# Messages' products directly behind the distances, and the first batch's imaginary parts added by TensorE

## The chip, the cores and the metric

The kernel runs on one core of a Trainium2 chip. The metric is the device time of one execution in microseconds, the median of several. Names used below: TensorE (PE in the profile) multiplies matrices into PSUM, whose banks of 512 numbers per partition the kernel takes from a pool of eight; VectorE (DVE), ScalarE (ACT) and GpSimd (POOL) work on what lies in SBUF and PSUM (GpSimd on SBUF alone); SyncE's queue (SP) issues most of the loads. Each engine has its own list of instructions, which the program writes by hand in a fixed order, and works through it from the front.

## The reference

There are 64 graphs of 256 nodes with 256 features. Layer 0 has three branches per graph, a convolution along the nodes (17 taps), a message passing with weights from distances, and a GRU that joins them; layer 1 is a graph convolution. Cut to what matters here:

```python
# layer 0
h = relu(bn(conv1d(x, conv1_w)))                  # 1 tap
h = bn(conv1d(h, conv2_w, pad=8))                 # 17 taps
x_conv = relu(h + x)
s    = x @ w_se.T + b_se                          # 3 numbers per node
dist = |s_n|^2 + |s_m|^2 - 2 s_n . s_m
A    = exp(-dist) * adj
msg  = relu(x @ w_msg.T + b_msg)
x_nmp = A @ msg
gi = concat(x_conv, x_nmp) @ w_ih.T + b_ih ;  gh = x @ w_hh.T + b_hh
r, z = sigmoid(gi_r + gh_r), sigmoid(gi_z + gh_z)
n = tanh(gi_n + r * gh_n)
x = layernorm(x + (1 - z) * n + z * x)
# layer 1
h = layer_norm(x) * gamma + beta
conv = (adj @ h) @ W_rel + b_rel + h @ W_root
x = layernorm(x + x + relu(conv))
```

## The kernel before

The 17-tap convolution is done for a batch of 8 graphs at a time by a polynomial transform: the nodes are cut into pieces, VectorE splits them into 15 complex "leaves" and two real ones (additions and multiply-adds, `split` and `merge`), TensorE multiplies each complex leaf with three filters, and VectorE puts the results together again. Of the three products of a leaf, k1 is the one of the sum of both parts; the real part is k1 minus the third product and the imaginary part is k1 plus the second. Two leaves share a bank per kind:

```python
    psum = ctx.enter_context(tc.tile_pool(name="psum", bufs=8, space=bass.MemoryType.PSUM))
    def bank(name):
        return psum.tile([P, 512], F32, tag="ps", name=name)

    def product(ps, slot, w, m):
        for c in range(C):                         # C = 2
            nc.tensor.matmul(ps, X[:, slot, c * P:(c + 1) * P], w(m, c), start=(c == 0), stop=(c == C - 1))   # L385

    def products(b, first, sums):
        p1, p2, p3 = bank("ps_k1"), bank("ps_k2"), bank("ps_k3")
        re, im, _ = LEAVES[first]
        for k in range(2):
            w = load_w(b, 3 * (first + k), 3)
            at = slice(k * D, (k + 1) * D)
            product(p1[:, at], sums + k, w, 0)
            product(p2[:, at], re + k, w, 1)
            product(p3[:, at], im + k, w, 2)
        def take():
            k1 = sl(sums, 2).rearrange("p s e -> p (s e)")
            nc.scalar.copy(k1, p1)                                                        # L400
            nc.vector.tensor_sub(sl(re, 2).rearrange("p s e -> p (s e)"), k1, p3)         # L401
            nc.vector.tensor_add(sl(im, 2).rearrange("p s e -> p (s e)"), k1, p2)         # L402
        return take
```

In the trace each float32 matmul is two instructions, so that `products` is 24 of them. `conv(b)` is a generator, which runs these pieces little by little: `take = products(...)`, some VectorE work, `take()`, and so on with the next pair of leaves. The first batch (b = 0) runs alone at the start, with the filters kept in SBUF; seven pairs and one odd group (`last_products`) are multiplied one after the other. It ends so:

```python
        if b == 0:
            def turned_x(q): ...         # 16 transposes of x into two banks (L541), left open for more
            yield None
            held = [turned_x(q) for q in range(3)]
        yield from butterflies([...])    # additions, L362
        for j in range(2): ...           # multiply-adds, L104
        ...
            for q in range(4):
                yield from second(q); yield from third(q); yield from third(q + 4)        # multiply-adds, L104
                pss = held.pop(0)
                ...                      # 16 transposes of the convolution's result onto x (L576)
                ...                      # relu by ScalarE (L581)
                if q == 1:
                    held.append(turned_x(3))
                yield None
```

The message part of a graph k, and the early calls for graphs 0 to 2:

```python
    def messages(k, idle=False):                   # idle: bias by TensorE, relu and copy by ScalarE
        ...
        for m in range(C):
            ps = bank("ps_msg")
            for c in range(C):
                nc.tensor.matmul(ps[:, :D + 4], XT[k][:, c, m * P:(m + 1) * P], wms[:, c, :], ...)   # L649
            if idle:
                ...
                continue
            nc.vector.tensor_add(twice[:, m, :, 0:3], ...)                 # L656, the 3 numbers s
            nc.vector.tensor_add(MSG[k][:, m, :], ps[:, :D], bms[:, :D])   # L658
        if not idle:
            nc.scalar.activation(MSG[k], MSG[k], AF.Relu)                  # L660
        ...                                        # five small GpSimd steps: -|s|^2 (L664 to L668)

    def factors(k): ...      # transposes of s (L675), two ScalarE copies
    def distances(k): ...    # two banks ps_dist, 2 products (L687), exponentials by ScalarE (L689)
    def mask(k): ...         # A = exp * adj by VectorE (L692)
    def passing(k): ...      # A @ msg (L699), copy by ScalarE

    while STAGE.get(0) != "inverse":               # the first batch's products
        if next(first) is None:
            count += 1
            if count == 3:   messages(0, True)
            elif count == 4: messages(1, True)
            elif count == 5: factors(0)
            elif count == 6: distances(0)
    messages(2, True)
    ...
    early = {2: lambda: factors(1), 3: lambda: mask(0), 4: lambda: passing(0)}
    for i, _ in enumerate(first):                  # the rest of the first batch
        if i in early:
            early[i]()
    distances(1)
    mask(1)
```

The main loop goes through the graphs of a batch, while `pump()` lets the next batch's convolution go on by its share. The end of an item (one graph k):

```python
            gates_n(k, 1)                  # bank ps_n, added by VectorE (L730)
            pump()
            project(k - 1)                 # two banks ps_out (L884), held until the aggregation
            distances(k + 2)
            step(up)                       # update: nn by VectorE twice, tanh by ScalarE
            pump()
            step(up)                       # update: w (from L839 on), statistics
            pump()
            messages(k + 3)
            step(up)                       # update: normalized h and x1
            pump()
            mask(k + 2)
            agg = aggregate(k - 1)         # L896 into the banks ps_out, added by VectorE (L898)
            step(agg)
            step(agg)
            pump()
```

Of the kernel before, what the change touches and what calls it, by code (L numbers as in the profile page):

```python
# [16 lines left out]
P = 128  # L17
# [59 lines left out]
def gnn_two_layers(  # L77
# [22 lines left out]
    def bank(name):  # L100
        return psum.tile([P, 512], F32, tag="ps", name=name)
# [278 lines left out]
        nc.sync.dma_start(out=t[:, :n], in_=w2m[first:first + n].rearrange("f c p o -> p f c o"))  # L380
        return lambda m, c: t[:, m, c, :]

    def product(ps, slot, w, m):
        for c in range(C):
            nc.tensor.matmul(ps, X[:, slot, c * P:(c + 1) * P], w(m, c), start=(c == 0), stop=(c == C - 1))  # L385

    def products(b, first, sums):

        p1, p2, p3 = bank("ps_k1"), bank("ps_k2"), bank("ps_k3")
        re, im, _ = LEAVES[first]  # L390
        for k in range(2):
# [8 lines that stand above are left out]
            nc.scalar.copy(k1, p1)  # L400
            nc.vector.tensor_sub(sl(re, 2).rearrange("p s e -> p (s e)"), k1, p3)  # L401
            nc.vector.tensor_add(sl(im, 2).rearrange("p s e -> p (s e)"), k1, p2)  # L402
        return take

    def last_products(b):
# [29 lines left out]
    def conv(b):  # L435
# [98 lines left out]
        if b == 0:  # L534

            def turned_x(q):
                xb = FIRST["xb"][q] if q < 3 else x_by_tiles(b, slice(q, M, 4))
                pss = [bank("ps_xc") for _ in range(C)]
                for o in range(C):
                    for j in range(4):  # L540
                        nc.tensor.matmul(pss[o][:, j * P:(j + 1) * P], xb[:, j, o * P:(o + 1) * P], ident,  # L541
                                         start=(j == 0), stop=False)
                return pss

            yield None
            held = [turned_x(q) for q in range(3)]
        yield from butterflies([(S2, U, U + 1, 1, True), (S2 + 1, U, U + 1, 1, False),
                                (U, S2, U + 2, 2, True), (U + 2, S2, U + 2, 2, False)])
        for j in range(2):
            stt(sl(S2 + j, 2, 2), sl(U + 4 + j, 2, 2), s4[j], sl(U + j, 2, 2))  # L550
            yield cost(2)
            stt(sl(S2 + 4 + j, 2, 2), sl(U + 4 + j, 2, 2), -s4[j], sl(U + j, 2, 2))
            yield cost(2)
# [14 lines left out]
        if b == 0:  # L568
            for q in range(4):
                yield from second(q)  # L570
                yield from third(q)
                yield from third(q + 4)
                pss = held.pop(0)
                for o in range(C):
                    for j in range(4):
                        nc.tensor.matmul(pss[o][:, j * P:(j + 1) * P], X[:, V + q + 4 * j, o * P:(o + 1) * P], ident,  # L576
                                         start=False, stop=(j == 3))
                for o in range(C):
                    pv = pss[o].rearrange("p (j g t) -> p j g t", j=4, g=BG)
                    for h in range(2):  # L580
                        nc.scalar.activation(xcs[h][:, o].rearrange("p g (t j) -> p j g t", j=M)[:, q::4],  # L581
                                             pv[:, :, 4 * h:4 * h + 4, :], AF.Relu)
                if q == 1:
                    held.append(turned_x(3))
                yield None
            return
        for j in range(4):
# [53 lines left out]
    def messages(k, idle=False):  # L641

        MSG[k] = ahead.tile([P, C, D], F32, tag="msg", name="msg", bufs=3)
        st = sts[k % len(sts)]
        twice = st.rearrange("p m (r e) -> p m r e", e=SR)
        for m in range(C):
            ps = bank("ps_msg")
            for c in range(C):
                nc.tensor.matmul(ps[:, :D + 4], XT[k][:, c, m * P:(m + 1) * P], wms[:, c, :],  # L649
                                 start=(c == 0), stop=(c == C - 1 and not idle))  # L650
            if idle:
                nc.tensor.matmul(ps[:, :D + 4], ones[0:1, :], bms[0:1, :], start=False, stop=True)
                nc.scalar.copy(twice[:, m, :, 0:3], ps[:, D:D + 3].unsqueeze(1).to_broadcast([P, 2, 3]))
                nc.scalar.activation(MSG[k][:, m, :], ps[:, :D], AF.Relu)
                continue
            nc.vector.tensor_add(twice[:, m, :, 0:3], ps[:, D:D + 3].unsqueeze(1).to_broadcast([P, 2, 3]),  # L656
                                 bms[:, D:D + 3].unsqueeze(1).to_broadcast([P, 2, 3]))
# [4 lines that stand above are left out]
        sq = ahead.tile([P, C, 3], F32, tag="sq", name="sq", bufs=2)  # L662
        ns = ahead.tile([P, C], F32, tag="ns", name="ns", bufs=3)
        nc.gpsimd.tensor_mul(sq, st[:, :, 0:3], st[:, :, 0:3])  # L664
        nc.gpsimd.tensor_add(ns, sq[:, :, 0], sq[:, :, 1])
        nc.gpsimd.tensor_add(ns, ns, sq[:, :, 2])
        nc.gpsimd.tensor_scalar(twice[:, :, :, 3], ns.unsqueeze(2).to_broadcast([P, C, 2]), -0.5, None, ALU.mult)
        nc.gpsimd.tensor_scalar(ns, ns, -1.0, None, ALU.mult)  # L668
        ST[k] = (st, ns)

    def factors(k):
        st, ns = ST[k]
# [35 lines left out]
    def gates_rz(k, n):  # L708
        if n == 0:
            RZ[k] = (work.tile([P, C, 2 * D], F32, tag="rz", name="rz", bufs=1),  # L710
                     work.tile([P, C, 2 * D], F32, tag="gn", name="gn", bufs=1))
        q, ins = inputs(k, n)
        prz = bank("ps_rz")
        for c in range(C):
            nc.tensor.matmul(prz, XT[k][:, c, q], whh[:, c, 0:2 * D], start=(c == 0), stop=False)  # L715
        for i, t in enumerate(ins):
            nc.tensor.matmul(prz, t, wih[:, i, 0:2 * D], start=False, stop=(i == 3))  # L717
        rz = RZ[k][0]

        nc.vector.tensor_add(rz[:, n, :], prz, brzn[:, :2 * D])  # L720
        nc.scalar.activation(rz[:, n, :], rz[:, n, :], AF.Tanh, scale=0.5)  # L721
# [379 lines left out]
    while STAGE.get(0) != "inverse":  # L1101
        if next(first) is None:
            count += 1
            if count == 3:
                messages(0, True)
            elif count == 4:
                messages(1, True)
            elif count == 5:
                factors(0)
            elif count == 6:  # L1110
                distances(0)
    messages(2, True)
    first_pool.close()

    work = ctx.enter_context(tc.tile_pool(name="work", bufs=2))
# [5 lines left out]
    nc.gpsimd.tensor_add(brzn[:, :2 * D], brzn[:, :2 * D], bhh)  # L1121
    load_x(0)

    early = {2: lambda: factors(1), 3: lambda: mask(0), 4: lambda: passing(0)}
    for i, _ in enumerate(first):
        if i in early:
            early[i]()
    distances(1)
    mask(1)

    POINTS = 10
# [3 lines left out]
    for b in range(NB):  # L1135
# [19 lines left out]
        for k in range(b * BG, min((b + 1) * BG, B - 1)):  # L1155
            load(k + 3)
            load_x(k + 1)
            up = update(k)
            agg = None
            gates_rz(k, 0)  # L1160
            pump()
            gates_n(k, 0)
            step(y_left)
            pump()
            if k > 0:
                transposes_h(k - 1)
            pump()
            gates_rz(k, 1)
            pump()
            if k + 1 < B:  # L1170
                passing(k + 1)
            pump()
            if k + 2 < B:
                factors(k + 2)
            gates_n(k, 1)
            pump()
            if k > 0:
                project(k - 1)
            if k + 2 < B:
                distances(k + 2)  # L1180
            step(up)
            pump()
            step(up)
            pump()
            if k + 3 < B:
                messages(k + 3)
            step(up)
            pump()
            if k + 2 < B:
                mask(k + 2)  # L1190
            if k > 0:
                agg = aggregate(k - 1)
# [3 lines that stand above are left out]
            y_left = agg  # L1196
# [7 lines left out]
    for k in range(first_k, B - 1):  # L1204
# [15 lines left out]
        project(k - 1)  # L1220
        if k + 2 < B:
            distances(k + 2)
        step(up)
        step(up)
        if k + 2 < B:
            block_sums(k + 1, 1)
        if k + 3 < B:
            messages(k + 3)
        step(up)
        if k + 2 < B:  # L1230
            mask(k + 2)
# [48 lines left out]
```

## Time and profile before

| | |
|---|---|
| median of 3 runs | 2248.66 us (2246.59 to 2248.96) |
| span of the profiled run | 2246.3 us |
| TensorE clock granted | 0.998 |
| mean DMA rate over the span | 101 GB/s |
| instructions | 24617 |

In the groups of instructions a line gives the source line, the engine, what is written from what, the shape, the number, the busy time and the mean of one. Those of the parts in question:

```profile
L649 PE MATMUL ps_msg<-wms,xT 128*128 128x260 f32 x512 | 131.4, 394 | 20.3 <-DVE XF L401 20.3
L699 PE MATMUL ps_nmp<-AT,msg 128*128 128x256 f32 x512 | 121.1, 379 | 0.0
L385 PE MATMUL ps_k<-w,XF 128*128 128x256 f32 x1316 | 294.2, 381 | 3.2 <-DMA w<-w2m 1.9
```

The last numbers are the time that the engine stood idle just before such instructions, and what ended it. A matmul's duration is that of one instruction through the pipe; in a stream the next one starts earlier than this one ends, so the time that TensorE needs is read from the starts. The chain of work that ended last runs for 84% of the span over TensorE and for 12% over VectorE.

### The profile page before, as it was taken

What the parts mean: (1) busy time and instruction counts of PE and PEld (TensorE: products, weight loads), DVE (VectorE), ACT (ScalarE), POOL (GpSimd) and SP (SyncE); (2) the same over time, 40 slices, a digit from 0 to 9 for tenths busy, and PEclk for the clock granted to TensorE, in tenths of its full rate; (3) what the DMA queues carried; (4) which work ended last, traced back from release to release, by engine and by line L of the source; (5) the groups of instructions that cost most, each with busy time, mean ns of one, the idle gap of its engine ahead of it and who ended that gap; (6) DMA issues with size and microseconds to landing.
All of it is one profiled execution on the core that took longest, in us unless ns stands there. A gap on an engine that the chain in (4) does not pass through costs nothing.

```text
span 2246.3 us, 24617 instructions
## 1 busy us (share of the span) xinstructions
PE 2202.2 (98%) x8400; PEld 1463.0 (65%) x8400; DVE 1721.5 (77%) x3329; ACT 769.2 (34%) x1587; POOL 511.7 (23%) x933
## 2 busy tenths in 40 slices
PE   8999999999999999999999999999999999999998
PEld 5775666656665666656666667666666667666664
DVE  6976889389882998749886598956989479896675
ACT  6423222532235322443224432244222432224333
POOL 0102212231221321223212321222212232222112
PEclk9999999999999999999999999999999999999999
DMA  5932433214423153232522244221432314421110
GB/s 149 316 111 69 141 103 98 96 46 140 136 76 103 38 164 108 78 106 80 164 64 84 92 132 131 70 97 64 142 111 83 103 54 141 131 81 38 43 33 19
DMA packets 212682, 226.69 MB, mean 101 GB/s; under 512 B 22103, under 2 KB 203854, under 8 KB 212558
## 3 DMA queue, kind: packets, MB, share of 16 engines
q1 hardware_dynamic: 190128, 191.27, 26.6%
q10 hardware_dynamic: 22430, 33.86, 4.3%
q8 instruction: 67, 1.10, 0.2%
q14 instruction: 57, 0.47, 0.1%
HBM read 179.22 MB, written 45.88 MB: 100 GB/s over the span
## 4 chain that ended last, share of the span: by engine, by line
PE 84%; DVE 12%; DMA 1%; issue 1%; POOL 1%; ACT 1%; SPq 0%; POOLq 0%; ACTq 0%; DVEq 0%
PE ps_rz L717 16%; PE ps_k L385 10%; PE ps_rz L715 8%; PE ps_n L729 8%; PE ps_out L884 7%; PE ps_c L468 5%; PE ps_nmp L699 5%; PE ps_msg L649 5%; PE ps_out L896 4%; PE ps_n L727 4%; DVE XF L104 4%; PE ps_w L230 2%; PE ps_dist L687 1%; DMA w<-w2m 1%; PE ps_hT L871 1%; DVE w L104 1%
## 5 line engine op out<-in xcount | busy, mean ns | idle before, releaser
L104 DVE SCALAR_TENSOR_TENSOR XF<-XF 128x512 f32<-128x512 f32 (+2 forms) x800 | 507.6, 665 | 7.4
L848 POOL TENSOR_SCALAR q<-mv 128x2 f32<-128x2 f32 x63 | 45.5, 723 | 1395.1 <-DVE mv L827 1395.1
L385 PE MATMUL ps_k<-w,XF 128*128 128x256 f32 x1316 | 294.2, 381 | 3.2 <-DMA w<-w2m 1.9
L385 PEld LDWEIGHTS ps_k<-w,XF 128*128 128x128 f32 x1316 | 247.9, 190 | 44.3 <-PE ps_n L729 6.2
L884 PE MATMUL ps_out<-wrr,hT 128*128 128x512 f32 x504 | 226.6, 592 | 0.0
L721 ACT ACTIVATE rz<-rz 128x512 f32<-128x512 f32 x114 | 71.9, 630 | 450.0 <-DVE rz L720 442.3
L730 DVE TENSOR_TENSOR gn<-ps_n,brzn 128x512 f32<-128x512 f32 x114 | 78.3, 687 | 181.3 <-PE ps_n L729 181.3
L715 PE MATMUL ps_rz<-whh,xT 128*128 128x512 f32 x456 | 214.5, 593 | 0.0
L717 PE MATMUL ps_rz<-wih,nmp 128*128 128x512 f32 x456 | 214.3, 592 | 0.0
L717 PE MATMUL ps_rz<-wih,xc 128*128 128x512 f32 x456 | 214.3, 592 | 0.0
L660 ACT ACTIVATE msg<-msg 128x512 f32<-128x512 f32 x61 | 38.4, 630 | 379.3 <-DVE msg L658 379.3
L720 DVE TENSOR_TENSOR rz<-ps_rz,brzn 128x512 f32<-128x512 f32 x114 | 77.6, 681 | 117.8 <-PE ps_rz L717 117.7
L717 PEld LDWEIGHTS ps_rz<-wih,xc 128*128 128x128 f32 x456 | 86.6, 190 | 109.1 <-issue 108.8
L717 PEld LDWEIGHTS ps_rz<-wih,nmp 128*128 128x128 f32 x456 | 86.6, 190 | 109.1 <-issue 109.1
L884 PEld LDWEIGHTS ps_out<-wrr,hT 128*128 128x128 f32 x504 | 95.3, 190 | 93.3 <-issue 81.3
L649 PE MATMUL ps_msg<-wms,xT 128*128 128x260 f32 x512 | 131.4, 394 | 20.3 <-DVE XF L401 20.3
L649 PEld LDWEIGHTS ps_msg<-wms,xT 128*128 128x128 f32 x512 | 92.6, 189 | 54.7 <-DVE XF L401 26.0
L362 DVE TENSOR_TENSOR XF<-XF 128x512 f32<-128x512 f32 (+3 forms) x128 | 126.2, 1010 | 1.7
L699 PE MATMUL ps_nmp<-AT,msg 128*128 128x256 f32 x512 | 121.1, 379 | 0.0
L715 PEld LDWEIGHTS ps_rz<-whh,xT 128*128 128x128 f32 x456 | 82.1, 190 | 57.7 <-issue 54.5
L896 PE MATMUL ps_out<-hr,adj 128*128 128x256 f32 x504 | 119.5, 380 | 0.0
L468 PE MATMUL ps_c<-xTc,w 128*128 128x512 f32 x256 | 116.7, 599 | 2.4 <-ACT xTc L458 2.3
(197 smaller groups left out, 3769.9 us busy)
## 6 DMA issues: line engine op xcount, KB each, us to landing
w<-w2m SPq DMA_DIRECT2D x105, 768.0 KB, 5.7
xn<-in_x_dram SPq DMA_DIRECT2D x32, 512.0 KB, 4.3
xt<-xTc ACTq DMA_DIRECT2D x32, 512.0 KB, 3.4
xT<-xt SPq DMA_DIRECT2D x64, 256.0 KB, 2.9
xb<-in_x_dram SPq DMA_DIRECT2D x32, 512.0 KB, 6.4
adj<-in_adjT_dram SPq DMA_DIRECT2D x64, 256.0 KB, 2.7
x<-in_x_dram SPq DMA_DIRECT2D x64, 256.0 KB, 3.0
out_dram<-y ACTq DMA_DIRECT2D x63, 256.0 KB, 2.2
```

Of the source, the lines that this page charges most:

```text
L104: nc.vector.scalar_tensor_tensor(o, in0, s, in1, op0=op0, op1=op1)
L362: (nc.vector.tensor_add if add else nc.vector.tensor_sub)(sl(o, n), sl(a, n), sl(b, n))
L385: nc.tensor.matmul(ps, X[:, slot, c * P:(c + 1) * P], w(m, c), start=(c == 0), stop=(c == C - 1))
L468: nc.tensor.matmul(pss[o], w1[:, c, o * P:(o + 1) * P], xTc[:, c, :], start=(c == 0), stop=(c == C - 1))
L649: nc.tensor.matmul(ps[:, :D + 4], XT[k][:, c, m * P:(m + 1) * P], wms[:, c, :], start=(c == 0), stop=(c == C - 1 and not idle))
L699: nc.tensor.matmul(ps[:, d * N:(d + 1) * N], MSG[k][:, m, d * P:(d + 1) * P], AT[k][:, m, :], start=(m == 0), stop=(m == C - 1))
L715: nc.tensor.matmul(prz, XT[k][:, c, q], whh[:, c, 0:2 * D], start=(c == 0), stop=False)
L717: nc.tensor.matmul(prz, t, wih[:, i, 0:2 * D], start=False, stop=(i == 3))
L727: nc.tensor.matmul(pn[:, D:], XT[k][:, c, q], whh[:, c, 2 * D:], start=(c == 0), stop=(c == C - 1))
L729: nc.tensor.matmul(pn[:, :D], t, wih[:, i, 2 * D:], start=(i == 0), stop=(i == 3))
L884: nc.tensor.matmul(ps, hT[:, c, n * P:(n + 1) * P], wrr[:, c, :], start=(c == 0), stop=(c == C - 1))
L896: nc.tensor.matmul(po, ADJ[k][:, m, n * P:(n + 1) * P], hr[:, m, :], start=False, stop=(m == C - 1), skip_group_check=True)
```

## The change

It has three parts. In the main loop, and in the last batch's loop, `messages` becomes a generator of two steps: the products come directly behind the distances, and the additions, the relu and the GpSimd steps come after the first pump, before the second step of the update. That is meant to take the products out of the place where they wait for a bank. In the first batch, the second product of a pair of leaves is accumulated onto k1 in its bank after k1 has been copied, so that the imaginary part is a copy by ScalarE in place of an addition by VectorE, and a pair takes two banks. And the early work of the first batch is put into another order, so that TensorE has something to do while VectorE finishes that batch. For graph 0 the GRU's products with the messages come before those with the convolution.

```diff
-    def product(ps, slot, w, m):
+    def product(ps, slot, w, m, first=True):
         for c in range(C):
-            nc.tensor.matmul(ps, X[...], w(m, c), start=(c == 0), stop=(c == C - 1))
+            nc.tensor.matmul(ps, X[...], w(m, c), start=first and c == 0, stop=(c == C - 1), skip_group_check=True)

     def products(b, first, sums):
+        if b == 0:
+            return products_added(first, sums)
...
+    def products_added(first, sums):
+        p1, p3 = bank("ps_k1"), bank("ps_k3")
+        re, im, _ = LEAVES[first]
+        w = [load_w(0, 3 * (first + k), 3) for k in range(2)]
+        at = [slice(k * D, (k + 1) * D) for k in range(2)]
+        k1 = sl(sums, 2).rearrange("p s e -> p (s e)")
+        for k in range(2):
+            product(p1[:, at[k]], sums + k, w[k], 0, k == 0)
+        nc.scalar.copy(k1, p1)
+        for k in range(2):
+            product(p3[:, at[k]], im + k, w[k], 2)
+        for k in range(2):
+            product(p1[:, at[k]], re + k, w[k], 1, False)
+        def take():
+            nc.scalar.copy(sl(im, 2).rearrange("p s e -> p (s e)"), p1)
+            nc.vector.tensor_sub(sl(re, 2).rearrange("p s e -> p (s e)"), k1, p3)
+        return take
...
-            held = [turned_x(q) for q in range(3)]
+            held = [turned_x(0)]
         yield from butterflies([...])
+        if b == 0:
+            FIRST["passing"]()                       # mask(0), passing(0)
+            held += [turned_x(q) for q in range(1, 3)]
...
                 if q == 1:
                     held.append(turned_x(3))
+                elif q == 2:
+                    FIRST["distances"]()             # distances(1)
...
     def messages(k, idle=False):
-        for m in range(C):
-            ps = bank("ps_msg")
+        pss = [bank("ps_msg") for _ in range(C)]
+        for m, ps in enumerate(pss):
             (products)
+        yield
+        for m, ps in enumerate(pss):
             (additions; behind them the relu and the GpSimd steps)
+        yield
...
-        for i, t in enumerate(ins):
-            nc.tensor.matmul(prz, t, wih[:, i, 0:2 * D], start=False, stop=(i == 3))
+        for j, i in enumerate((2, 3, 0, 1) if k == 0 else range(4)):
+            nc.tensor.matmul(prz, ins[i], wih[:, i, 0:2 * D], start=False, stop=(j == 3))
...
-            if count == 3:
-                messages(0, True)
-            elif count == 4:
-                messages(1, True)
+            if count == 4:
+                all_of(messages(0, True))
...
-    messages(2, True)
+    all_of(messages(1, True))
+    all_of(messages(2, True))
...
-    early = {2: lambda: factors(1), 3: lambda: mask(0), 4: lambda: passing(0)}
-    (the rest of the first batch with these calls in between; then distances(1))
+    factors(1)
+    (the rest of the first batch, with passing(0) and distances(1) inside it)
     mask(1)
...
             distances(k + 2)
+            msg = messages(k + 3) if k + 3 < B else None
+            step(msg)
             step(up)
             pump()
+            step(msg)
             step(up)
             pump()
-            if k + 3 < B:
-                messages(k + 3)
             step(up)
             pump()
```

The loop of the last batch is changed in the same way, without pumps.

## The prediction, made before the changed kernel was run

> **What bounds the kernel now.** I read the busy times first, then the waits of TensorE alone, then its timeline around each wait with VectorE's timeline for the same microseconds. TensorE bounds it:
>
> ```profile
> PE 2202.2 (98%) x8400; PEld 1463.0 (65%) x8400; DVE 1721.5 (77%) x3329; ACT 769.2 (34%) x1587; POOL 511.7 (23%) x933
> ...
> PE ps_msg L649 <- DVE XF L401: 20.3, 14, 1.6
> PE ps_xc L576 <- DVE XF L104: 3.4, 1, 3.4
> ```
>
> The change adds and removes no matmul, so it can win only time in which TensorE stands still, and the reader sees in lines 2 and 3 that little of that is there: 14 waits of the message products (the columns are total, number, longest) and one wait in the first batch. The first of the 14, and the second, which is shaped a little differently, in TensorE's timeline:
>
> ```profile
> 282.12 0.70 PE L687 MATMUL ps_dist<-lr 4*128 4x256 f32 x4
> 282.75 5.45 PE L385 MATMUL ps_k<-w,XF 128*128 128x256 f32 x24
> 288.03 1.04 PE L649 MATMUL ps_msg<-wms,xT 128*128 128x260 f32 x4
> 290.68 1.14 PE L649 MATMUL ps_msg<-wms,xT 128*128 128x260 f32 x4 [1.60 <-DVE XF L401]
> ...
> 325.14 0.70 PE L687 MATMUL ps_dist<-lr 4*128 4x256 f32 x4
> 325.77 5.45 PE L385 MATMUL ps_k<-w,XF 128*128 128x256 f32 x24
> 331.05 1.04 PE L649 MATMUL ps_msg<-wms,xT 128*128 128x260 f32 x4
> 333.38 1.14 PE L649 MATMUL ps_msg<-wms,xT 128*128 128x260 f32 x4 [1.28 <-DVE XF L401]
> ```
>
> Starts are what to read, since durations overlap: 24 product instructions advance TensorE by 288.03 - 282.75 = 5.28 us, 0.22 each, and so does a message instruction. Four of them from 288.03 end at 288.91; the next starts at 290.68, 1.77 us late. In the second case 331.05 + 0.88 = 331.93 against 333.38, 1.45 late. The pair comes once in each of seven batches at nearly the same sizes (14 waits in the list), so the stalls are worth 7 x (1.77 + 1.45) = **22.5 us**, a bit more than the 20.3 that is listed as wait, because the pipe refills.
>
> What is waited for is a bank. PSUM has eight here, and the pool hands out the one released longest ago, in the order of the program. At this point the two output products hold two banks until the aggregation, the two distance tiles two, the n gate one, and the conv product issued one item earlier (I call it A) three, as VectorE hasn't taken its results. The next conv product (B) takes the bank of the n gate and those of the distances; for the messages only A's are left, and the second of them is free when L401 has run. VectorE is behind:
>
> ```profile
> 282.51 0.68 DVE L104 SCALAR_TENSOR_TENSOR nn<-rz,gn 128x512 f32<-128x512 f32 x1
> 283.23 0.69 DVE L104 SCALAR_TENSOR_TENSOR nn<-nn,gn 128x512 f32<-128x512 f32 x1
> 283.84 2.15 DVE L362 TENSOR_TENSOR XF<-XF 128x1024 f32<-128x1024 f32 x3
> ...
> 289.94 0.68 DVE L401 TENSOR_TENSOR XF<-XF,ps_k 128x512 f32<-128x512 f32 x1
> ...
> 291.55 0.41 DVE L658 TENSOR_TENSOR msg<-ps_msg,bms 128x256 f32<-128x256 f32 x1
> ...
> 328.81 0.68 DVE L839 TENSOR_TENSOR w<-x,nn 128x512 f32<-128x512 f32 x1
> ```
>
> The reader sees the order: first step of the update (nn, twice), the first pump's conv work (L362), the second step (w, from 285.91), then L401 at 289.94. The last line is where the second step begins in the second case. In the first batch:
>
> ```profile
> 105.43 0.69 DVE L401 TENSOR_TENSOR XF<-XF,ps_k 128x512 f32<-128x512 f32 x1 [1.94 <-PE ps_k L385]
> 106.04 0.68 DVE L402 TENSOR_TENSOR XF<-XF,ps_k 128x512 f32<-128x512 f32 x1
> ...
> 138.55 1.99 PE L699 MATMUL ps_nmp<-AT,msg 128*128 128x256 f32 x8
> 143.95 5.53 PE L576 MATMUL ps_xc<-ident,XF 128*128 128x128 f32 x32 [3.41 <-DVE XF L104]
> ```
>
> From 105.43 VectorE works without a pause to the combinations that L576 transposes. TensorE has run out of other work at about 140.4 and starts L576 at 143.95: 3.6 us lost. The 32 transposes then take 5.4 us to the next group (149.32) where 32 x 0.11 = 3.5 would do, since each quarter waits for its own combinations: 1.8 more, **5.4 us** in all.
>
> **What the Trainium skill says.** Perfetto Trace Analysis, section Optimization Strategy: the same gap coming back on the engine that should be saturated can mean that there is no SBUF or PSUM for the next tile. The trace agrees: 14 gaps of 1.45 or 1.77 us, all ended by the release of a bank. PSUM — Partial Sum Buffer, section Engine vs sequencer instructions: ScalarE and VectorE take their instructions strictly in order, and matmuls start in program order. This carries the prediction, since a bank is free only when VectorE reaches its reader, and one waiting matmul holds up all behind it; the trace agrees, as the aggregation's L896, which needs no new bank, comes only after the late message product. The same page, section The four PSUM rules: a matmul without the first flag adds to what the bank holds. The first batch's new products rest on that; no run shown yet has it for this tile.
>
> **The change, part by part.**
>
> 1. *Message products directly behind the distances, additions before the update's second step.* TensorE's work is the same: 8 x 0.22 + 0.1 = 1.85 us move ahead of B. In 40 of the other 47 items nothing stands between distances and messages, and in 7 only products of the first convolution, whose banks were copied long before; I expect nothing there. In the 14 items the banks are dealt out anew. Messages 0 and 1 get the n gate's bank and that of the first distance tile (its exponential ends well before message 1 starts: 282.85 + 0.42 = 283.27 against 283.6). So the 22.5 us go. But B now gets the second distance bank and then, as A's are released later in the program, the banks of messages 0 and 1. B's first tile needs four instructions, then its second tile must wait until VectorE has added message 0. First case: B starts at 282.75 + 1.85 = 284.60, its second tile is due at 284.60 + 0.86 = 285.46. VectorE reaches the additions behind the first pump at 285.91; the small one (0.08 to the next start) and L658 (0.41) end at 286.40, and TensorE starts some 0.06 later (before, 290.62 to 290.68). Stall 286.46 - 285.46 = 1.00. Second case: 325.77 + 1.85 + 0.86 = 328.48 against 328.81 + 0.55 = 329.36: 0.88. The third tile follows 0.86 later and message 1 is added 0.41 after message 0, so it doesn't wait. New stalls 7 x (1.00 + 0.88) = 13.2 us. Net 22.5 - 13.2 = **9.3 us** won.
>
> ScalarE's relu of the messages now stands in front of A's copy (L400), which ends near 288 instead of 285.06; L401 is at about 290.7 (0.8 later by the additions put before it), so that costs nothing.
>
> 2. *First batch, imaginary parts by TensorE.* Seven additions L402 leave VectorE, 0.61 us each from start to start: 4.3 us, of which four (2.4 us) lie behind 105.43 in the chain to L576. Seven ScalarE copies of about 0.58 us come in, on an engine that has pauses of 3 us between such copies there. TensorE's third product must wait until k1 has been copied out of the same bank: the copy takes 0.2 + 0.58, and the product between, 8 x 0.216 = 1.73 us, hides it. Two banks instead of three per product only eases.
>
> 3. *First batch, order.* The messages of graph 0 come one product later. Product 3 ended at 105.3 only because 3.3 us of messages were ahead of it; now it ends near 102, and VectorE's chain starts 3.7 us earlier (105.43 to 101.7). With part 2 the combinations are ready 3.7 + 2.4 = 6.1 us earlier, at about 137.8. Messages 1 (3.3 us) go behind the last product and become filler: TensorE's last product ends at 125.8 instead of 129.5 (from 80.95: 188 x 0.216 = 40.6, one graph's messages 3.3, factors and distances 0.9), then two messages (6.6), the factors, one group of turned x (1.8), passing (1.7), two more groups (3.5), to about 140. The combinations wait for TensorE now, by 2 us, and the following quarters too. So the 5.4 us go, less about 0.3 for the factors of graph 1, whose scalars pass through four GpSimd steps (1.1 to 3.5 us in the three cases of the trace) against 3.3 us of other messages: **5.1 us**.
>
> Sum: 9.3 + 5.1 = 14.4; 2248.66 - 14.4 = **2234 us**.
>
> **Rivals.** (a) *No new wait for banks*: if B's second tile could have A's first bank (free at 285.06 in the trace before), the message stalls would go almost whole: 22.5 + 5.1, about 2221 us. For it: VectorE has 23% to spare. Against: the program's order of release. (b) *The wait is handed on undiminished*: if B's third tile got A's L401 bank it would be due at 286.3 and wait over 4 us; 14 such waits, 56 us, would make it 2277. Against: the additions are released earlier in the program than A's results. A milder form, additions held up by another microsecond, leaves only the first batch: 2243. (c) *The first batch gives nothing*, because adj or the factors come late: 2239 with part 1 as above. For it: adj's transfers start only when the filters' memory is free, and take 2.6 to 9.4 us. Against: 2 us of slack.
>
> **Range and chances.** TensorE's starts at its steady pace add up to about 2184 us, so even without any pause the gain were below 3%, and 2% (45 us) would need twice all the stalls in reach. 2% slower needs rival (b) in full. I give the sum 60%, (a) 15%, the milder (b) or (c) 23%. The range 2225 to 2242 holds most of that. Faster by over 2%: 0.02, within 2%: 0.96, slower by over 2%: 0.02.
>
> **What would show it.** Right: TensorE's wait of message products on L401 is gone; 14 waits of about 1 us appear at a conv product, ended by L658; first message, then B in the timeline; L576 without a wait; L402 seven fewer. Wrong: no such waits (rival a), waits on L401 at L385 (rival b), L576 or the factors waiting in the first batch (c), or any wait in the other 47 items, for which I expect none.

## The result, and the profile after

The changed kernel takes 2247.7 us (median of 4 runs, 2246.7 to 2248.9); the kernel before took 2248.8 beside it. The ratio is 0.9997, with a 95% interval from 0.998 to 1.0015: no difference that can be measured, where 14 us were predicted. Both things that the change was made for did happen, and at nearly the sizes predicted; the time went elsewhere.

The first line is the page's busy times, the second its chain of the work that ended last:

```profile
PE 2205.1 (98%) x8400; PEld 1459.6 (65%) x8400; DVE 1719.0 (76%) x3322; ACT 773.1 (34%) x1594; POOL 503.8 (22%) x933
...
PE 67%; DVE 24%; DMA 3%; issue 3%; POOL 2%; ACT 1%; SPq 0%; POOLq 0%; DVEq 0%; ACTq 0%
```

TensorE still bounds the kernel. But the chain runs over VectorE for 24% of the span, where it was 12%, and over DMA for 3%. These are TensorE's waits after the change (total, number, longest):

```profile
PE ps_k L386 <- DVE st L688: 12.0, 14, 0.9
PE ps_a L826 <- DVE XF L831: 7.7, 7, 1.8
PE ps_k L386 <- DMA w<-w2m: 4.7, 12, 1.1
```

The 14 message waits and the wait of the first batch are gone. The first line here is the bank wait that was foreseen in their place. The second and the third are new in size: 1.8 us in one wait, and 1.9 us, in the kernel before.

**The 14 items.** TensorE's timeline of the changed kernel at the first of them, and then VectorE's:

```profile
276.09 0.70 PE L724 MATMUL ps_dist<-lr 4*128 4x256 f32 x4
276.72 2.02 PE L678 MATMUL ps_msg<-wms,xT 128*128 128x260 f32 x8
278.58 1.03 PE L386 MATMUL ps_k<-w,XF 128*128 128x256 f32 x4
280.52 4.55 PE L386 MATMUL ps_k<-w,XF 128*128 128x256 f32 x20 [0.92 <-DVE st L688]
```

```profile
277.81 2.16 DVE L362 TENSOR_TENSOR XF<-XF 128x1024 f32<-128x1024 f32 x3
279.89 0.16 DVE L688 TENSOR_TENSOR st<-ps_msg,bms 128x6 f32<-128x6 f32 x1
279.96 0.42 DVE L690 TENSOR_TENSOR msg<-ps_msg,bms 128x256 f32<-128x256 f32 x1
280.29 0.16 DVE L688 TENSOR_TENSOR st<-ps_msg,bms 128x6 f32<-128x6 f32 x1
280.36 0.42 DVE L690 TENSOR_TENSOR msg<-ps_msg,bms 128x256 f32<-128x256 f32 x1
280.69 0.69 DVE L877 TENSOR_TENSOR w<-x,nn 128x512 f32<-128x512 f32 x1
```

Four product instructions from 278.58 end at 279.44, and the fifth, which needs the bank of message 0, starts at 280.52: 1.08 us late, right after message 0 has been added (L690, until 280.38). The listing names the small addition, which reads the same bank. In the second item of each batch the pause is 0.95. So 7 x (1.08 + 0.95) = 14.2 us have replaced the 22.5, 8.3 won.

**The first batch.** TensorE has no pause there any more:

```profile
126.43 1.04 PE L678 MATMUL ps_msg<-wms,xT 128*128 128x260 f32 x4
...
135.16 1.89 PE L736 MATMUL ps_nmp<-AT,msg 128*128 128x256 f32 x8
136.89 3.73 PE L565 MATMUL ps_xc<-ident,xb 128*128 128x128 f32 x32
140.46 3.74 PE L603 MATMUL ps_xc<-ident,XF 128*128 128x128 f32 x32
```

The 32 transposes follow the turned x at once and take 3.58 us, to the next group at 144.04. Behind the first batch the layer 1 products (L922) start 5.8 us earlier than in the kernel before.

**Where it was given back.** I followed the starts of those layer 1 products, one per item, in both traces. The lead of 5.8 us after the first batch rises and falls with each later batch and is 6.4 at the end of the main loop, though 8.3 more should have come in there: 7.7 were lost. Then, towards the end, the lead goes 6.3, 5.1, 4.2, 3.2, 2.2, 1.2, 0.2, and it ends as a loss of 0.8: 7.2 more are lost. Of the seven steps of about 1 us, the first two belong to the main loop's last two items (counted here and not in the 7.7), the other five to the items of the last batch's loop that have messages. 5.8 + 8.3 - 7.7 - 7.2 = -0.8. VectorE in one of the last batch's items, before and after:

```profile
2088.19 0.69 DVE L104 SCALAR_TENSOR_TENSOR nn<-nn,XF 128x512 f32<-128x512 f32 x1
2090.44 0.69 DVE L839 TENSOR_TENSOR w<-x,nn 128x512 f32<-128x512 f32 x1 [1.56 <-ACT nn L835]
...
2094.61 0.16 DVE L656 TENSOR_TENSOR st<-ps_msg,bms 128x6 f32<-128x6 f32 x1
...
2095.61 0.74 DVE L858 TENSOR_SCALAR h<-w,mv,q 128x256 f32<-128x256 f32 x2
```

```profile
2085.02 0.69 DVE L104 SCALAR_TENSOR_TENSOR nn<-nn,XF 128x512 f32<-128x512 f32 x1
2086.97 0.17 DVE L688 TENSOR_TENSOR st<-ps_msg,bms 128x6 f32<-128x6 f32 x1 [1.26 <-PE ps_msg L678]
...
2088.26 0.68 DVE L877 TENSOR_TENSOR w<-x,nn 128x512 f32<-128x512 f32 x1
...
2093.43 0.73 DVE L896 TENSOR_SCALAR h<-w,mv,q 128x256 f32<-128x256 f32 x2 [0.93 <-POOL q L888]
```

Before, w waited 1.56 us for the tanh and started 2.25 after the start of the second nn. Now VectorE is held by the additions, which themselves wait 1.26 for the message products, and w starts 3.24 after it: **1.0 us later**. The additions used to lie between w's statistics and h, where they filled the time in which GpSimd makes the scale q; now that time is a wait of 0.93. So VectorE does the same work, but the item's own chain (w, statistics, q, h, and on TensorE hT and the next item) is longer by a microsecond, and towards the end, when the convolutions are done, TensorE has nothing else to do: six of L826's waits are new, (7.7 - 1.8) / 6 = 1.0 us each.

In the main loop other work covers most of this. What isn't covered goes through a load. SyncE's queue takes its loads in order, and the load of the next x into one of two buffers waits until w has been read from that buffer. The queue before, and after, at loads of one kind (L639 and L668 are x, L380 the filters of the convolution):

```profile
786.58 0.38 SPq L634 DMA_DIRECT2D adj<-in_adjT_dram  x1
787.76 0.37 SPq L639 DMA_DIRECT2D x<-in_x_dram  x1
788.18 11.68 SPq L380 DMA_DIRECT2D w<-w2m  x5
```

```profile
778.68 0.38 SPq L663 DMA_DIRECT2D adj<-in_adjT_dram  x1
781.41 0.37 SPq L668 DMA_DIRECT2D x<-in_x_dram  x1
781.83 16.42 SPq L380 DMA_DIRECT2D w<-w2m  x7
```

From adj to x it takes 2.73 us where it took 1.18, as x must wait for the w that starts at 780.69, and the filters stand behind x. Their products were due at 786.2 and start at 787.21; before, they start at 794.12 without a pause. (The listing names a VectorE step beside that pause, which the product doesn't read; the second and the third filter of this load land at 789.3 and 791.5, 2.2 apart, which puts the first at 787.1.) In the list of SyncE's waits, those for w grew from 60.1 us in 14 to 81.3 in 18.

### The profile page after: what moved, and what is told of

It is laid out like the page before. It is cut to its first block, busy times and chain, and to the rows that moved or that the text cites. A ratio compares the mean times of both kernels' runs of the same rounds, so it can differ in the third digit from the quotient of the medians.

```text
span 2247.1 us, 24777 instructions
## 1 busy us (share of the span) xinstructions
PE 2205.1 (98%) x8400; PEld 1459.6 (65%) x8400; DVE 1719.0 (76%) x3322; ACT 773.1 (34%) x1594; POOL 503.8 (22%) x933
## 4 chain that ended last, share of the span: by engine, by line
PE 67%; DVE 24%; DMA 3%; issue 3%; POOL 2%; ACT 1%; SPq 0%; POOLq 0%; DVEq 0%; ACTq 0%
PE ps_k L386 14%; PE ps_rz L755 11%; DVE XF L104 9%; PE ps_rz L752 6%; PE ps_n L767 6%; PE ps_out L922 5%; PE ps_c L492 5%; PE ps_nmp L736 4%; DMA w<-w2m 3%; PE ps_msg L678 3%; PE ps_n L765 3%; PE ps_out L934 3%; DVE XF L362 2%; DVE XF L456 2%; DVE nn L104 1%
## 5 line engine op out<-in xcount | busy, mean ns | idle before, releaser
L696 POOL TENSOR_TENSOR sq<-st 128x6 f32<-128x6 f32 x64 | 13.8, 215 | 1219.2 <-DVE st L688 1169.3
L922 PE MATMUL ps_out<-wrr,hT 128*128 128x512 f32 x504 | 226.7, 592 | 0.0
L899 ACT ACTIVATE x<-w,sh,q 128x256 f32<-128x256 f32 x126 | 68.8, 593 | 342.7 <-POOL sh L891 342.7
L922 PEld LDWEIGHTS ps_out<-wrr,hT 128*128 128x128 f32 x504 | 95.2, 190 | 93.6 <-issue 81.8
L765 PE MATMUL ps_n<-whh,xT 128*128 128x256 f32 x456 | 117.2, 379 | 0.0
```

Of the source, the lines that this page charges most:

```text
L765: nc.tensor.matmul(pn[:, D:], XT[k][:, c, q], whh[:, c, 2 * D:], start=(c == 0), stop=(c == C - 1))
L922: nc.tensor.matmul(ps, hT[:, c, n * P:(n + 1) * P], wrr[:, c, :], start=(c == 0), stop=(c == C - 1))
```

## The experiments

All ratios are to the kernel before, run on the same chip beside each, with 95% intervals. Its own median was 2248.0 to 2248.8 us on these chips, so a difference between the times of two experiments can be off by about 1 us for that alone. "The first batch's part" means parts 2 and 3 of the change together.

**1. The first batch's part alone.** The messages stay whole at their old place in both loops:

```diff
-            msg = messages(k + 3) ...; step(msg); step(up); pump(); step(msg); step(up); pump(); step(up)
+            step(up); pump(); step(up); pump(); all_of(messages(k + 3)); step(up)
```

> Changed first batch alone; in both loops the messages stand whole at their old place, behind the second pump. Theory (gains and losses add up): the first batch's 5.8 us stay to the end, 2243.0 us, and the 14 waits of message products on L401 are back (22 us in the gaps). Rival (whatever TensorE wins early is given back to VectorE or the transfers later): 2247 to 2248.

2241.5 us, ratio 0.997 [0.9958, 0.9981]. Its first and third line of waits:

```profile
PE ps_msg L678 <- DVE XF L405: 20.3, 14, 1.6
...
PE ps_a L826 <- DVE XF L831: 1.8, 1, 1.8
```

The message waits are back as they were, and the new waits of the last batch are gone: they belong to the split of the messages. Added to the first batch's part, that split costs 6 us.

**2. The last batch's loop as before**, the rest changed.

> The changed kernel, but in the last batch's loop the additions go back behind the second step of the update (TensorE's order is the same there). Theory: the additions ahead of w delay VectorE by 1 us per item and TensorE then waits for the first gate sum; the seven waits of 1.2 us at ps_a go back to about 0.2, 2247.7 - 7 = 2240.7. Rival (the last batch is late because of the bank order or GpSimd): 2247, waits stay.

2242.8 us, ratio 0.9973 [0.9963, 0.9983]. L826's waits fall from 7.7 in 7 to 2.7 in 2, and 4.9 us come back. The edit reaches the five items of the last batch's loop, at 1.0 us each. The other 2.3 of the 7.2 belong to the main loop's last two items, which it leaves as they are, as the one wait that stays.

**3. Split only in the two items of a batch that had the wait.** In the other six, and in the last batch, the messages stay whole at their old place:

```diff
+            apart = k % BG in (3, 4)
-            step(msg); step(up); pump(); step(msg); step(up); pump(); step(up)
+            if apart: step(msg)
+            step(up); pump()
+            if apart: step(msg)
+            step(up); pump()
+            if not apart: all_of(msg)
+            step(up)
```

> Messages split only in the two items of a batch (k mod 8 = 3 and 4) in which a convolution product stood between distances and messages; old place in all others, last batch old. Theory: 5.8 from the first batch and 8.3 from the banks (22.5 less the 14.2 of new waits on L688), 2248.8 - 14.1 = 2234.7, up to 2237 if the additions still delay transfers in these two items. Rival (given back): 2240 or above.

2232.2 us, ratio 0.993 [0.9918, 0.9943]. Against experiment 2 the main loop's other items give 10.6 us, where the starts put the loss at 7.7 and 2.3 for the last two items: in the main loop the split lost more than the 8.3 that it won.

**4. As 3, with the additions directly behind the update's first step**, in front of the first pump, so that B's second tile finds its bank free.

> As the run before, but in the two items the additions come directly behind the update's first step, ahead of the first pump. Theory: the two message banks are free some 2 us earlier, before TensorE asks for them, so the 14 waits of about 1 us at the product go too: 2248.8 - 5.8 - 22.5 = 2220.5, with VectorE's delay at most 2224. Rival (VectorE waits for the message products and all behind it is late): no faster than the run before, 2235.

2220.0 us, ratio 0.9876 [0.9863, 0.989], the best of all. Its timeline of TensorE at the same item:

```profile
276.60 0.70 PE L724 MATMUL ps_dist<-lr 4*128 4x256 f32 x4
277.23 2.02 PE L678 MATMUL ps_msg<-wms,xT 128*128 128x260 f32 x8
279.09 5.34 PE L386 MATMUL ps_k<-w,XF 128*128 128x256 f32 x24
284.27 1.89 PE L934 MATMUL ps_out<-hr,adj 128*128 128x256 f32 x8
```

All 24 product instructions run in one piece: 284.27 - 279.09 = 5.18 us. The bank wait that replaced the old one wasn't inherent; it came from 2.16 us of convolution work that stood in front of the additions.

**5. Products early, additions left at their old place**, behind w, in all items.

> The changed kernel with the products directly behind the distances as in it, but the additions at their old place, behind the second pump, in both loops. If a bank goes to the one that asks next in the program's order of release, the product B gets the banks of A now: its third tile waits for L401, about 4 us in each of the 14 items (58 us in place of 14), while the last batch's 7 us and about 8 us of transfers come back: 2248 + 44 - 15 = 2277. If the banks don't matter and only the place of the products does: 2233 or less.

2305.6 us, ratio 1.0263 [1.0247, 1.0278]. TensorE's timeline, and then the windows of the same stretch (window, its length, busy time and number of PE, PEld, DVE, ACT and POOL, granted clock, DMA share, GB/s):

```profile
279.08 1.89 PE L386 MATMUL ps_k<-w,XF 128*128 128x256 f32 x8
285.15 5.31 PE L386 MATMUL ps_k<-w,XF 128*128 128x256 f32 x16 [4.18 <-DVE XF L405]
290.29 1.89 PE L934 MATMUL ps_out<-hr,adj 128*128 128x256 f32 x8
```

```profile
280.00:284.00 4.00, 0.97 (x5) 0.51 (x3) 3.83 (x10) 0.00 (x0) 0.19 (x1) 1.00 0.00 0
284.00:287.00 3.00, 1.85 (x4) 1.51 (x5) 2.97 (x10) 0.14 (x1) 2.41 (x7) 0.66 0.00 0
287.00:290.00 3.00, 3.00 (x12) 2.54 (x11) 2.96 (x9) 1.48 (x3) 2.44 (x4) 0.77 0.00 0
```

This is what the prediction's rival (b) describes. Eight instructions from 279.08 end at 280.81 and the next starts at 285.15: 4.34 us late, 4.02 in the second item, 58.5 us in all. That is the bank rule, to 5%. But the time went up by 57.6, although 5.8 from the first batch and the old 22.5 are gone from it, so 57.6 + 5.8 + 22.5 - 58.5 = 27.4 more were lost. TensorE's starts show 24 of them at the same places: the 16 instructions behind this pause take 290.29 - 285.15 = 5.14 us where 3.46 would do, as the granted clock falls to 0.66 and 0.77. Where the other 3 us went is not shown. The Trainium skill (TensorE: Matmul & The Clock Gate, section What's actually happening) says that the clock is halved until work releases it, with an activity window of about 3.4 us; the trace agrees: the first seven instructions behind the pause take 0.43 us or more each, and from the ninth on 0.22. Two results hang on this run besides. The products stand early in all items, and L826's waits are down to 1.8 in one: so it is the additions' place, not the products', that delays the last batch. And the filters' waits are 1.4 us in 4.

**6. A third buffer for x** in the changed kernel, so that its load need not wait for w.

```diff
-            x = work.tile([P, C, D], F32, tag="x", name="x")
+            x = work.tile([P, C, D], F32, tag="x", name="x", bufs=3)
```

> The changed kernel with three buffers in place of two for the graphs' x (the memory is that of a row of biases, used once before). Theory (the additions ahead of w keep the x buffer in use longer, so the queue issues the filters' loads later, and TensorE waits for them): the gaps between the n gate's products and a convolution product, 8.1 us, shrink to 3 or less, about 2243; the last batch's seven waits stay. Rival (transfers are late for another reason): 2247, gaps stay.

2244.1 us, ratio 0.9983 [0.9975, 0.999]. The filters' waits:

```profile
PE ps_k L386 <- DMA w<-w2m: 1.8, 4, 0.5
```

12 waits become 4, and the pauses of TensorE between the n gate and the next product fall from 8.1 us to 3.7; they were 4.6 in the kernel before. The last batch is as in the changed kernel (L826 waits 7.7 us in 7). So the load behind x is one way of the loss in the main loop, some 3.6 us of the 7.7. That size is uncertain: it is 3.1 by the ratios, whose intervals overlap, and 4.4 by the pauses.

**7 and 8. The first batch's order alone, and its imaginary parts alone**, with the messages as before.

> First batch's new order alone: three products with three banks and the imaginary parts added by VectorE as before; messages whole at their old place. By the prediction's sums VectorE's chain is ready 3.7 us earlier and TensorE has 3.3 us more filler: together more than the 3.6 us wait, so nearly all of the first batch's gain: 2248.8 - 5 = 2244 (the run with both parts has 2241.5).

> The kernel before with the imaginary parts added by TensorE alone, all orders old. VectorE has 0.61 us less to do in each of four pairs behind the point from which it doesn't pause: 2.4 us off the wait of 3.6 us, the quarters' waits of 1.8 us stay: 2248.8 - 2.4 = 2246.4. If the copy's wait within the bank costs TensorE anything, 2248 or more.

2245.2 us, ratio 0.9986 [0.998, 0.9993], and 2245.3, ratio 0.9987 [0.9981, 0.9994]. Each gives about 2.7 us, both 6.7 by experiment 1. With the order alone TensorE waits 1.6 us at the passing (L734), since VectorE is late with the mask; with the imaginary parts alone 1.7 in two waits at the transposes (L600). They are two halves of one thing, VectorE ready earlier and TensorE with filler until then, and neither half closes the pause. The intervals are too wide to say whether they add up to more than 5.4.

**9. As 4, with the third buffer for x.**

> Messages split in two items of each batch only, their additions right behind the update's first step, and a third buffer for x. If the third buffer helped the changed kernel (3.6 us) because the additions let go of x late in most items, it has little to do here, where w is delayed in two items of eight: 2218 to 2220 us, against 2220 without it. If the third buffer is worth its 3.6 us in itself, about 2216.

2221.5 us, ratio 0.9876 [0.986, 0.9891], the same as without it. A third buffer is worth something only where w is late.

**10. The changed kernel with the additions early in all items**, as in 4 for two.

```diff
             step(msg)
             step(up)
+            step(msg)
             pump()
-            step(msg)
             step(up)
```

> The changed kernel with the additions right behind the update's first step, in front of the first pump, in all items of both loops. No product waits for L688 any more: of the 14.2 us of the changed kernel at least 13 go. If what was lost elsewhere came from w being a microsecond later, it stays, since the additions are still in front of w: the last batch's waits at the aggregated features, about 7 us, and the late filters and h of the main loop, 6 to 10; 2231 to 2236 us. If it came from something else, such as the place of the products or of the relu behind the pump, about 2220, as with two items of eight.

2235.2 us, ratio 0.9938 [0.9926, 0.9951]. Its first waits of TensorE:

```profile
PE ps_a L826 <- DVE XF L831: 8.6, 7, 1.8
PE ps_k L386 <- DMA w<-w2m: 3.0, 7, 1.0
```

No product waits for L688 any more, and the last batch waits as in the changed kernel. Against experiment 4 only the other items and the last batch differ: 15 us (14 by the ratios) for the split in those, with additions in front of w where nothing called for them.

## Why the prediction was wrong

**Step 1, the 14 items: right.** The banks went where the rule of release put them. Predicted were 1.00 and 0.88 us, measured 1.08 and 0.95; net 8.3 won instead of 9.3. VectorE was as far along as foreseen: it ended the additions of message 0 1.80 and 1.67 us after B's start, in the sums 1.80 and 1.68. But TensorE started 0.14 us behind that end, where 0.06 had been put.

**Step 1, "I expect nothing there": this is the step that failed.** It looked at the products only. In the other 47 items their move was indeed nearly free: in experiment 5 the last batch loses nothing by it. But the additions moved too, from behind w to in front of it. I had read VectorE as an engine with 23% to spare and asked only when it releases banks; I didn't ask what stands behind the additions in its list. That is w, at the head of the item's own chain: about 1 us later each time. It took most of the 7.2 us at the end, where little hides it, and of the 7.7 in the main loop, some 3.6 of them by way of the loads behind x. Experiments 2, 3 and 6 each take away one piece of it, and 10, which takes away the bank waits alone, leaves it.

Of the other 4 us of the main loop, TensorE's starts show 2.9 at the turning of h (hT), in one item of each of six batches. The kernel before, and then the changed one:

```profile
496.88 1.03 PE L729 MATMUL ps_n<-wih,nmp 128*128 128x256 f32 x4
497.74 0.60 PE L871 MATMUL ps_hT<-ident,h 128*128 128x128 f32 x4
498.18 1.88 PE L715 MATMUL ps_rz<-whh,xT 128*128 128x512 f32 x4
```

```profile
489.38 1.03 PE L767 MATMUL ps_n<-wih,nmp 128*128 128x256 f32 x4
490.55 0.78 PE L909 MATMUL ps_hT<-ident,h 128*128 128x128 f32 x4
491.16 1.88 PE L752 MATMUL ps_rz<-whh,xT 128*128 128x512 f32 x4
```

From the first to the third line it takes 1.78 us instead of 1.30, 0.48 more. It is 1.30 in experiment 3, 1.41 in experiment 5 (products early, additions late) and 1.78 in experiment 10, so most of it comes with the additions in front of w. The last us is not accounted for. Nor is one pause near the end, 1.46 us instead of 0.84 at one item's distances: experiment 4 has it too, so it isn't the split of that item.

**Steps 2 and 3, the first batch: right in size (5.8 us by the trace, 6.7 by experiment 1, 5.1 predicted), wrong in one cause.** I put 1.8 us of it down to each quarter of the transposes waiting for its own combinations. The windows of the kernel before show another:

```profile
143.70:147.00 3.30, 3.05 (x13) 2.95 (x14) 3.23 (x6) 0.76 (x2) 0.00 (x0) 0.53 0.76 245
147.00:149.30 2.30, 2.30 (x21) 2.30 (x20) 2.23 (x5) 1.88 (x5) 0.00 (x0) 0.93 0.01 4
```

Behind the pause of 3.6 us the granted clock is 0.53, and the transposes take 0.21 us each instead of 0.11 for 3.3 us. The pause had cost half as much again; with it, that went too.

**The rivals.** (a) is what experiment 4 reached, by another way: not a lucky bank, but earlier additions. Of (b) the milder form, which leaves the first batch's gain alone (2243 us), came nearest in size but not in cause: in the 14 items no addition came late, and the gain was lost in items without a bank wait. In full (b) was priced at 56 us of waits, 2277 us; experiment 5 had such waits and took 2306, most of the difference through the clock. The 2% were never near, as said.

## What to carry to other kernels

When work is moved to release something sooner, ask for every item in which it moves, not only those with the wait, what now stands behind it in its engine's list; an engine with spare time over the whole still has an urgent order within an item. Cure a wait only where it occurs: split in two of eight items and with the additions at the head of VectorE's work, the same idea is worth 28 us instead of 1, the first batch's part counted in both. And find every holder of a buffer on a load queue: a reader that is 1 us late can hold up the load behind its own.

## What the runs showed of the hardware that was not expected

In these runs a pause of TensorE of 3.6 us or more mostly cost more than its length. In experiment 5 there are 14 pauses of 4.02 to 4.34 us. Of these, 12 were followed by six to nine 256-column instructions at 0.43 us or thereabouts instead of 0.22, one by eleven and one by none: 24 us in all, 1.7 each on the average. In the kernel before, the 3.6 us of the first batch were followed by 3.3 us at a clock of 0.53. The one pause without a loss is as long as others with one:

```profile
1450.80 3.72 PE L386 MATMUL ps_k<-w,XF 128*128 128x256 f32 x16 [3.86 <-DVE XF L405]
```

The trace's record of the granted clock has half the clock in stretches of 3.41 us (once 6.83), which start on one regular grid whatever the pauses. This pause lies across two steps of the grid, with 1.42 and 1.55 us of TensorE's work in them; but one with the usual loss (its end at 891.12) lies almost alike, with 1.52 and 1.44, so why this one cost nothing stays open. Behind the shorter pauses there is no such loss: not behind those of 1.77 us in the kernel before, and behind the 1.08 us of the changed kernel the 20 instructions take 284.91 - 280.52 = 4.39 us, 0.22 each.
